# Two neighbouring 128x512 squares turned by one 128x1024 DVE instruction in an attention layer

## The chip, the cores and the metric

One Trainium2 chip, one core. The metric is the device time of one execution in microseconds (us), from the first to the last instruction of the program with what lies around it; a kernel's time is the median of its runs. The engines are named as in the profile: PE (matrix products), PEld (its weight loads), DVE, ACT and POOL (elementwise work), SP (which issues the transfers here). Each takes its own instructions in a fixed order and waits at one until its inputs are there.

## What is computed

32 graphs of 512 nodes with 256 features go through four layers, each of the form `x = x + layer(relu(layernorm(x)))`. Layers 0, 1 and 3 are graph attention layers; layer 2 is attention with eight heads of width 32. The change is in layer 2:

```python
qkv = jnp.einsum('fnc,ck->fnk', x, w_qkv)
q, k, v = jnp.split(qkv, 3, axis=-1)          # H = 8 heads, D = 32
scores = jnp.einsum('fnhd,fmhd->fhnm', q, k) / jnp.sqrt(jnp.asarray(D, x.dtype))
scores = jnp.where(adj > 0, scores, -1000000000.0)
attn = jax.nn.softmax(scores, axis=-1)
t = jnp.einsum('fhnm,fmhd->fnhd', attn, v).reshape(F, N, C)
```

Everything is in 32-bit floats.

## The kernel before

**How the work is ordered.** Class `Graph` writes down, graph by graph and layer by layer, the steps of the computation as ops: an engine, a length, what is read and written, and a function `emit` that issues the instructions. `Plan.order` then makes one list of all ops of all 32 graphs (up to six are in flight), by due times made of a period and of a table of shifts (`SHIFTS`), with buffers and banks handed out on the way. The ops' lengths are numbers written in the code (0.69 us for a square's transpose). The list is then emitted op by op, and each engine's instructions are held in that order. So the order on each engine is a product of the plan; the waits come from data: an instruction waits for the last writers and readers of what it touches.

**The attention layer.** `mha` runs twice per graph (`g`, four heads each, `PACK = 4`), and in it over pairs of node blocks (`c0 = 0, 2`), each with two blocks `c` of 128 nodes. For one block, in the order of the steps:

- PE, L1347: the four heads' scores, each 128x512, into four banks of PSUM.
- per head `h`: DVE, L1367, adds the mask and takes the smallest value, from the bank into the head's part of the buffer `p`; ACT, L1378, takes the exponential in place and sums it; DVE, L1386, turns each 32x32 square of the 128x512 part in place.
- SP, L1391: one store of the block's four heads to a page in device memory (`sheet`), then L1399, four loads from it into `pT`, which bring the squares to the other partitions. Each load waits for the store to land.

After two blocks PE, L1412, multiplies `pT` with `v` (16 products, 32 instructions); ACT copies the result (L1427), PE turns it (L1435) and DVE scales it by the sums (L1441, L1442).

`p` is one buffer of 128 partitions and, per partition, four node blocks `j`, two blocks `c`, four heads and 128 elements. A head's part is four runs of 128 elements; the parts of heads `h - 1` and `h` are neighbours, so that the two together are four runs of 256.

**Around it.** In steady state an engine's list mixes the layers of several graphs. Names that occur below: L586 and L587 (DVE, statistics of a layernorm), L791 (DVE, the masked maximum of a graph attention layer), L832 (DVE) and L840 (ACT, exponential) for its probabilities, L821 (POOL, bias), L859 (PE, a product with ones for the mean of a layer's rows), L694 (ACT, eviction with bias and relu), L704 (PE, a projection whose input L694 makes), L683 (PE, another projection), L720 (PE, rows made by transposes), L896 (DVE, the end of an elu), L1206, L1210 and L1297 (DVE, additions), L1523 (PE, products into a bank of four heads' sums), L1149 (DVE, reciprocals of sums), L809 (POOL, small arithmetic).

Only the heads that share a bank or buffer tie these layers together: PE can't write a bank of PSUM before DVE or ACT has read what was there.

The part of `mha` that is touched:

```python
def tile(h=h, c=c, p=p):
    return p[:, :, c % 2, h, :]
...
def emit(tile=tile):
    squared = tile().rearrange("p j (l i) -> p j l i", i=SQUARE)
    dve.transpose(squared, squared)

self.op("dve", 0.69, [part], [part, [(self, "done", n % 2, h)]], emit)
```

Of the kernel before, what the change touches and what calls it, by code (L numbers as in the profile page):

```python
# [50 lines left out]
SQUARE = 32  # L51
# [357 lines left out]
def adj_preln_kernel(  # L409
# [118 lines left out]
    pe, act, dve, pool = nc.tensor, nc.scalar, nc.vector, nc.gpsimd  # L528
    plan = Plan()

    def held(what, which):
        return [(what, which)]
# [10 lines left out]
    class Graph:  # L543
# [785 lines left out]
        def mha(self, g, qT, kT, v, y):  # L1329

            heads = [slice(h * MHA_DIM, (h + 1) * MHA_DIM) for h in range(PACK)]

            low = self.small(f"lows{g}", NC, PACK)
            sums = self.small(f"sums{g}", NC, PACK)
            rinv = self.small(f"rinvs{g}", NC, PACK)
            squares = P // SQUARE
            for c0 in range(0, NC, 2):

                p = Quad(NC, 2, PACK, P)
                sheet = Buffer("sheet", NC, 2, PACK * P)  # L1340
                pT = Quad(squares, 2, PACK, P)
                for c in (c0, c0 + 1):
                    sc = [Buffer("bank", N) for _ in range(PACK)]

                    def emit(c=c, sc=sc):
                        for h, d in enumerate(heads):
                            pe.matmul(  # L1347
                                sc[h].ap,
                                qT[d, g, c * P : (c + 1) * P],
                                kT[d, g, :],  # L1350
                                start=True,
                                stop=True,
                            )

                    n = g * NC + c
                    before = [(self, "done", n % 2, h) for h in range(PACK)]
                    reads = [qT.part(g), kT.part(g), before]
                    parts = [(p, c % 2, h) for h in range(PACK)]
                    self.op("pe", 1.14, reads, [*sc, parts], emit)
                    for h in range(PACK):  # L1360
                        part = [parts[h]]

                        def tile(h=h, c=c, p=p):
                            return p[:, :, c % 2, h, :]

                        def emit(h=h, c=c, sc=sc, tile=tile):
                            dve.tensor_tensor_reduce(  # L1367
                                tile(),
                                sc[h].ap.rearrange("p (j f) -> p j f", j=NC),
                                mask_bias[:, c, :].rearrange("p (j f) -> p j f", j=NC),  # L1370
                                -MHA_SCALE, HIGHEST,
                                op0=ALU.add, op1=ALU.min, accum_out=low[:, c, h : h + 1],
                            )

                        self.op("dve", 0.77, [sc[h], held("mask", c)], [part, low], emit)
                        self.op(
                            "act", 0.82, [part, low], [part, sums],
                            lambda h=h, c=c, tile=tile: act.activation(  # L1378
                                tile(), tile(), AF.Exp, scale=-1.0,
                                bias=low[:, c, h : h + 1], accum_out=sums[:, c, h : h + 1],  # L1380
                            ),
                        )

                        def emit(tile=tile):
                            squared = tile().rearrange("p j (l i) -> p j l i", i=SQUARE)
                            dve.transpose(squared, squared)  # L1386

                        self.op("dve", 0.69, [part], [part, [(self, "done", n % 2, h)]], emit)
                    self.transfer(
                        [parts], [[(sheet, c % 2)]], 1024,  # L1390
                        lambda c=c, p=p, sheet=sheet: nc.sync.dma_start(  # L1391
                            sheet[:, :, c % 2, :],
                            p[:, :, c % 2].rearrange("p j h f -> p j (h f)"),
                        ),
                    )
                    for to in range(squares):

                        def emit(c=c % 2, to=to, pT=pT, sheet=sheet):
                            nc.sync.dma_start(  # L1399
                                pT[to * SQUARE : (to + 1) * SQUARE, :, c].rearrange(  # L1400
                                    "p l h f -> p l (h f)"
                                ),
                                sheet[:, to, c].rearrange("(l p) f -> p l f", p=SQUARE),
                            )

                        self.transfer([[(sheet, c % 2)]], [[(pT, c % 2, to)]], 256, emit, True)
                acc = Buffer("bank", 2 * P)

                def emit(acc=acc, pT=pT):
                    for j in range(NC):  # L1410
                        for h, d in enumerate(heads):
                            pe.matmul(  # L1412
                                acc[d, :],
                                v[:, j, g * P + d.start : g * P + d.stop],
                                pT[:, :, :, h, j * SQUARE : (j + 1) * SQUARE].rearrange(
                                    "p l c i -> p c l i"
                                ),
                                start=(j == 0),
                                stop=(j == NC - 1),
                            )  # L1420

                reads = [(pT, c, to) for c in range(2) for to in range(squares)]
                r = Buffer("row", 2, P)
                self.op("pe", 1.97, [v, reads], [acc, r], emit)
                self.op(
                    "act", 0.4, [acc], [r],
                    lambda acc=acc, r=r: act.activation(  # L1427
                        r.ap.rearrange("p c i -> p (c i)"), acc.ap, AF.Copy
                    ),
                )  # L1430
                back = Buffer("bank", 2, PACK, MHA_DIM)

                def emit(r=r, back=back):
                    for i in range(2):
                        pe.transpose(back[:, i, :, :], r[:, i, :], ident)  # L1435

                self.op("pe", 0.27, [r], [back], emit)

                def emit(c0=c0, back=back):
                    cs = slice(c0, c0 + 2)  # L1440
                    dve.reciprocal(rinv[:, cs, :], sums[:, cs, :])  # L1441
                    dve.tensor_mul(  # L1442
                        y[:, cs, g * P : (g + 1) * P].rearrange("p c (h d) -> p c h d", h=PACK),
                        back.ap,
                        rinv[:, cs, :, None].to_broadcast([P, 2, PACK, MHA_DIM]),
                    )

                self.op("dve", 1.0, [back, sums], [rinv, y], emit)
# [199 lines left out]
```

## Time and profile before

| | |
|---|---|
| runs (3) | 4419.26, 4421.39, 4423.37 us; median 4421.39 |
| the profiled execution | 4422.42 us, of which its span 4420.6 |
| instructions in the span | 69315 |
| mean granted clock of PE | 0.979 |
| L1367, DVE, mask of one head | x1024, mean 674 ns |
| L1378, ACT, exponential of one head | x1024, mean 719 ns |
| L1391, store to the sheet | x256, 1024 KB, 5.3 us to landing |
| L1399, loads from it | x1024, 256 KB, 5.4 us to landing |
| L1412, PE | x4096, mean 395 ns |

How to read it: a page of the profile has a busy time per engine, a line of tenths for 40 equal slices of the span, and groups of instructions: line, engine, operation, what is written and read with its shape, count, busy time in us, mean ns of one, the idle time of the engine just in front of them, and what ended that idle time. A record of DVE is longer than the distance to the next one's start where two follow each other without a wait, since their ends overlap. A timeline lists instructions in order of time with the start (us from the span's start), length, engine, line and operation; "x4" is four merged; in brackets stands the idle time in front and what ended it. A view of waits sums who waited for whom. "Granted clock" is the share of full speed that PE's clock was given.

### The profile page before, as it was taken

The numbers are of one execution on the slowest core, as the hardware profiler recorded it, in microseconds if no ns is written. First come the engines' busy times: TensorE is split into PE (matmuls) and PEld (weight loads), VectorE is DVE, ScalarE is ACT, GpSimd is POOL, SyncE is SP. The second block draws the span as 40 slices with busy tenths as digits, with TensorE's granted clock in tenths as the row PEclk, the third lists the DMA queues.
The fourth block names the chain that finished last, engine by engine and source line by source line (L and its number), as shares of the span: only waits on it lengthen the run. The fifth ranks groups of instructions, "written<-read, shape, count | busy, mean of one in ns | idle before, by whom it ended". The sixth has DMA issues, their size and how long they took to land. (4 is left out here: it accounts for less than half of the span.)

```text
span 4420.6 us, 69315 instructions
## 1 busy us (share of the span) xinstructions
PE 4170.8 (94%) x21648; PEld 2583.3 (58%) x21648; DVE 3662.7 (83%) x9016; ACT 2924.3 (66%) x6309; POOL 3034.1 (69%) x3119
## 2 busy tenths in 40 slices
PE   6999999999999999999999999999999999999765
PEld 3656556665566666566666556666656666655332
DVE  3577888888888888888888888888889888888873
ACT  2556666777676667667667767666766766676653
POOL 1424766777776677776677777667777766777677
PEclk9999999999999999999999999999999999999877
DMA  3287667766767766766777667677667677766760
GB/s 121 84 226 218 187 190 220 218 202 181 215 199 211 224 200 201 204 204 194 222 215 204 201 200 211 194 224 210 205 205 206 192 217 219 201 200 186 231 175 29
DMA packets 441504, 867.22 MB, mean 196 GB/s; under 512 B 35248, under 2 KB 119728, under 8 KB 441136
## 3 DMA queue, kind: packets, MB, share of 16 engines
q1 hardware_dynamic: 439520, 862.78, 66.4%
q8 instruction: 173, 2.83, 0.3%
q14 instruction: 195, 1.60, 0.1%
q10 hardware_dynamic: 1616, 0.01, 0.0%
HBM read 443.23 MB, written 419.43 MB: 195 GB/s over the span
## 5 line engine op out<-in xcount | busy, mean ns | idle before, releaser
L1386 DVE STREAM_TRANSPOSE cells<-cells 128x512 f32<-128x512 f32 x1024 | 702.4, 698 | 148.8 <-ACT cells L1378 148.5
L1378 ACT ACTIVATE cells<-cells,smalls 128x512 f32<-128x512 f32 x1024 | 736.1, 719 | 114.0 <-DVE smalls L1367 105.8
L1367 DVE CUSTOM_DVE_ANT_0 cells<-bank,mask_bias 128x512 f32<-128x512 f32 x1024 | 686.9, 674 | 21.6 <-PE bank L1347 20.6
L821 POOL TENSOR_TENSOR cells<-mask_biasT,row 128x1024 f32<-128x1024 bf16 x320 | 682.3, 2155 | 16.2 <-ACT row L730 16.2
L791 DVE CUSTOM_DVE_ANT_0 masked<-bank,mask_bias 128x512 f32<-128x512 f32 x768 | 520.5, 678 | 71.1 <-PE bank L720 64.7
L683 PE MATMUL bank<-cells,mlp_sb 128*128 128x512 f32 x1024 | 473.1, 600 | 19.8 <-DMA cells<-page 13.2
L704 PE MATMUL bank<-fc_sb,cells 128*128 128x256 f32 (+1 forms) x2048 | 474.7, 381 | 1.5 <-DVE smalls L1367 0.8
L927 PE MATMUL bank<-cells 128*128 128x260 f32 x2048 | 465.1, 383 | 1.1 <-ACT cells L840 0.9
L603 ACT ACTIVATE cells<-cells,smalls 128x256 f32<-128x256 f32 x768 | 408.1, 592 | 74.7 <-POOL smalls L596 49.7
L1159 PE MATMUL bank<-cells 128*128 128x512 f32 x1024 | 450.9, 597 | 0.0
L927 PEld LDWEIGHTS bank<-cells 128*128 128x128 f32 x2048 | 387.9, 190 | 87.1 <-issue 24.9
L840 ACT ACTIVATE cells<-cells,smalls 128x512 f32<-128x512 f32 x512 | 348.5, 726 | 114.7 <-DVE cells L832 114.6
L704 PEld LDWEIGHTS bank<-fc_sb,cells 128*128 128x128 f32 x2048 | 376.9, 189 | 76.5 <-DVE cells L1442 19.0
L586 DVE BATCH_NORM_STATS2 smalls<-cells 128x6 f32<-128x256 f32 x768 | 311.3, 405 | 110.4 <-POOL cells L1222 101.3
L883 ACT ACTIVATE cells<-cells 128x512 f32<-128x512 f32 (+1 forms) x256 | 188.1, 735 | 292.9 <-DVE cells L946 111.3
L832 DVE SCALAR_TENSOR_TENSOR cells<-bank,smalls,cells 128x512 f32<-128x512 f32 x512 | 354.1, 740 | 30.5 <-POOL cells L821 27.0
L720 PEld LDWEIGHTS bank<-ident,smalls 128*128 128x128 f32 x2176 | 254.3, 141 | 212.6 <-issue 84.2
L720 PE MATMUL bank<-ident,smalls 128*128 128x128 f32 x2176 | 325.9, 284 | 54.2 <-POOL smalls L809 30.0
L1159 PEld LDWEIGHTS bank<-cells 128*128 128x128 f32 x1024 | 194.1, 193 | 230.2 <-issue 228.7
L1484 POOL TENSOR_TENSOR cells<-cells 128x1024 f32<-128x1024 f32 x128 | 302.3, 2372 | 19.2 <-PE bank L1502 8.4
L683 PEld LDWEIGHTS bank<-cells,mlp_sb 128*128 128x128 f32 x1024 | 186.0, 191 | 218.5 <-issue 170.3
L1347 PE MATMUL bank<-cells 32*128 32x512 f32 x2048 | 305.8, 644 | 5.7 <-DVE smalls L1367 4.8
(141 smaller groups left out, 8503.9 us busy)
## 6 DMA issues: line engine op xcount, KB each, us to landing
sheet<-cells SPq DMA_DIRECT2D x256, 1024.0 KB, 5.3
cells<-sheet SPq DMA_DIRECT2D x1024, 256.0 KB, 5.4
page<-cells SPq DMA_DIRECT2D x256, 512.0 KB, 3.4
cells<-page SPq DMA_DIRECT2D x192, 512.0 KB, 6.1
cells<-in_x_dram SPq DMA_DIRECT2D x64, 512.0 KB, 7.3
cells<-page SPq DMA_DIRECT2D x256, 128.0 KB, 2.9
out_dram<-cells SPq DMA_DIRECT2D x32, 512.0 KB, 5.4
mlp_sb<-in_L_gnn_mlp_w_dram SPq DMA_DIRECT2D x2, 512.0 KB, 6.7
```

Source lines behind the costliest of these rows:

```text
L603: lambda c=c: act.activation(xn[:, c, :], src[:, c, :], func, bias=off[:, c : c + 1], scale=rstd[:, c : c + 1],),
L683: lambda k=k, s=s, i=i, m=m, mm=mm: pe.matmul(mm.ap, w[:, k, cols + m * P : cols + (m + 1) * P], s.rows(i), start=(k == 0), stop=(k == nk ...
L704: pe.matmul(mm[:, :n], src[k // 2].nodes(k % 2, c), w[:, k, cols : cols + n], start=(k == 0), stop=(k == nk - 1),)
L720: pe.transpose(bc[:, c * P : (c + 1) * P], col(c).to_broadcast([P, P]), ident)
L791: lambda c=c: dve.tensor_tensor_reduce(masked, f2_ps.ap, bias[:, c, :], 1.0 - ALPHA, FLOOR, op0=ALU.add, op1=ALU.max, accum_out=top[:, c : ...
L821: lambda half=half: pool.tensor_add(p[half].ap, biasT[:, 2 * half : 2 * half + 2, :], w_row[:, None, :].to_broadcast([P, 2, N]),),
L832: lambda j=j, ph=ph, i=i: dve.scalar_tensor_tensor(ph[:, i, :], f1_ps.ap, term(2)[:, j : j + 1], ph[:, i, :], op0=ALU.max, op1=ALU.add,),
L927: pe.matmul(mm[:, :w1], p[j // 2][:, j % 2, c * P : (c + 1) * P], v[:, j, :], start=(j == 0), stop=(j == NC - 1),)
L1159: pe.matmul(mm.ap, h1[jh][:, i, m * P : (m + 1) * P], p[jh][:, i, :], start=(jh + i == 0), stop=(jh + i == 2),)
L1367: dve.tensor_tensor_reduce(tile(), sc[h].ap.rearrange("p (j f) -> p j f", j=NC), mask_bias[:, c, :].rearrange("p (j f) -> p j f", j=NC), - ...
L1378: lambda h=h, c=c, tile=tile: act.activation(tile(), tile(), AF.Exp, scale=-1.0, bias=low[:, c, h : h + 1], accum_out=sums[:, c, h : h + 1],),
L1386: dve.transpose(squared, squared)
```

## The change

For every odd head, one transpose turns the squares of the two heads `h - 1` and `h`; for an even head the op stays in the plan with its length, its reads and its writes, but issues nothing.

```diff
-                        def emit(tile=tile):
-                            squared = tile().rearrange("p j (l i) -> p j l i", i=SQUARE)
-                            dve.transpose(squared, squared)
+                        def emit(h=h, c=c, p=p):
+                            if h % 2:
+                                two = p[:, :, c % 2, h - 1 : h + 1, :].rearrange(
+                                    "p j h (l i) -> p j (h l) i", i=SQUARE
+                                )
+                                dve.transpose(two, two)
 
                         self.op("dve", 0.69, [part], [part, [(self, "done", n % 2, h)]], emit)
```

The ops' lengths, reads and writes are what they were, so the plan makes the same list. 1024 instructions of 128x512 become 512 of 128x1024. The odd head's instruction stands at the odd head's place in the list, wherever the even head's place is. The lines below the change move by three (L1389 is the new transpose, L1394 the store, L1402 the loads, L1415 the product).

## The prediction

> **What bounds the kernel now.** First the page, then the busy times of the engines by stage. The first fence has PE and the turned squares from the page; the second has three stages (start:end, length, then the busy time and instructions of PE, PEld, DVE, ACT and POOL, granted clock, DMA).
>
> ```profile
> PE 4170.8 (94%) x21648; PEld 2583.3 (58%) x21648; DVE 3662.7 (83%) x9016; ACT 2924.3 (66%) x6309; POOL 3034.1 (69%) x3119
> ...
> L1386 DVE STREAM_TRANSPOSE cells<-cells 128x512 f32<-128x512 f32 x1024 | 702.4, 698 | 148.8 <-ACT cells L1378 148.5
> ```
> ```profile
> 0.00:640.00 640.00, 568.55 (x2657) 359.19 (x2658) 430.86 (x1104) 347.72 (x733) 277.30 (x318) 0.97 0.59 172
> 640.00:3920.00 3280.00, 3221.53 (x17034) 2007.20 (x17034) 2868.78 (x7022) 2289.14 (x4970) 2393.64 (x2444) 1.00 0.70 206
> 3920.00:4420.00 500.00, 380.75 (x1962) 216.91 (x1958) 363.02 (x892) 287.39 (x608) 363.13 (x359) 0.87 0.57 165
> ```
>
> From 640 to 3920 us PE works 3221.5 of 3280 us (98.2%), DVE 87%. This is three quarters of the span: 26 rounds of one graph each, 129.2 to 134.1 us from one L1412 of graph g to that of g+1. PE takes its instructions in a fixed order, so in these rounds DVE's time costs nothing until a result comes later than PE needs it, and then PE loses all of the lateness. DVE's saving is not the question; DVE's order is. I therefore read the waits of PE (about 2 us a round: 20.6 us for L1297, 8.6 for L1149, 6.2 for L809 over the 18 rounds of 1170 to 3510) and then, row by row, DVE's timeline of one round, 2210 to 2342, and how long before PE's start each input was done.
>
> **Price of one wide instruction.** The trace has no 128x1024 transpose. The nearest rows are two narrow ones back to back, and L896, a 128x1024 f32 instruction from SBUF to SBUF:
>
> ```profile
> 3196.50 1.28 DVE L1386 STREAM_TRANSPOSE cells<-cells 128x512 f32<-128x512 f32 x2
> ```
> ```profile
> 3227.22 1.21 DVE L896 SCALAR_TENSOR_TENSOR cells<-cells 128x1024 f32<-128x1024 f32 x1
> ```
>
> L896 with 512 elements takes 0.68 at its shortest, so 512 more elements cost 0.53. The wide transpose is then 0.70 + 0.53 = 1.23 us, against 1.28 for the pair: merging saves some 0.06 us, 512 times 0.06 = 33 us of DVE in the whole run. Bounds of the wide one: 1.21 (L896) and 2 x 0.70 = 1.40 (no overlap at all). I take 1.23, since L896's two sizes show the slope directly and the transpose's own row shows the fixed part.
>
> The Trainium skill's "Perfetto Trace Analysis" (Identifying the Most-Contended Engine) says that matmul busy time is a bad measure of how near TensorE is to its limit, and that weight loads and useful work should be read instead; DVE is read by occupancy. Weight loads fill 61% of the middle stage, so by this rule DVE at 87% is the engine to shorten, and the sum would be a gain, 4422 - 33 = 4389. I go by the waits instead: PE's order is fixed, and it has no room whatever it does with its time.
>
> **What the change moves.** Every head keeps its place in DVE's order, but an even head's place issues nothing and the odd head's takes both. At an even place whatever follows starts 0.60 us earlier (the start to start of two narrow ones); after the odd place it is 0.53 later than that. Where DVE runs on without a wait the two cancel to -0.06. Two things break this. First, a wait between the two places eats the earliness and leaves +0.53. Second, the order of the four heads isn't always 0, 1, 2, 3: in 94 of 512 pairs the odd place comes first, so DVE is 0.53 late until the even one. In these 94 the even head's exponential was over at least 2.3 us before the odd place, so the change adds no new wait. On PE, ACT, POOL and SP the instructions and their order stay. Per round I find two places where the lateness meets PE.
>
> *Place one.* Heads go 0, 2, 3, 1. DVE waits for head 3's exponential, and both wide instructions come after that wait (columns: start us, length, engine, line):
>
> ```profile
> 2333.55 0.71 DVE L1386 STREAM_TRANSPOSE cells<-cells 128x512 f32<-128x512 f32 x1 [0.79 <-ACT cells L1378]
> 2334.34 0.43 DVE L586 BATCH_NORM_STATS2 smalls<-cells 128x6 f32<-128x256 f32 x1
> 2334.80 0.18 DVE L587 BATCH_NORM_AGGREGATE smalls<-smalls 128x2 f32<-128x6 f32 x1
> 2334.90 0.68 DVE L1386 STREAM_TRANSPOSE cells<-cells 128x512 f32<-128x512 f32 x1
> ```
>
> Everything behind 2334.90 is late by 2 x 0.53 = 1.07. Two queues carry it to PE. (a) L832 starts at 2336.03, ACT's L840 waits for it, and ACT's L694 (2338.41, after 0.25 idle) and its twin (end 2340.28) come behind: 1.07 - 0.25 less a few hundredths = 0.75 late. PE's L704 at 2340.32 starts 0.04 after that L694, in every round: PE loses 0.75. (b) SP issues the store to the sheet at 2335.67, 0.09 after the second transpose; its loads land at 2348.01 and PE's L1412 starts at 2348.47. In 9 of 26 rounds PE already waits here (0.17 to 0.91); there it loses the full 1.07. In the other 17 L1412 starts 0.51 to 0.88 after the landing, where the waiting ones start 0.24 after it (median), so the spare time is 0.27 to 0.64, the new wait 0.43 to 0.80, and (a) has mostly paid for it. Both start from the same lateness, so the larger counts: 17 x 0.75 + 9 x 1.07 = 22.4 us.
>
> *Place two* follows at once. Heads go 1, 3, 2, 0:
>
> ```profile
> 2351.64 0.71 DVE L1386 STREAM_TRANSPOSE cells<-cells 128x512 f32<-128x512 f32 x1
> 2352.27 0.65 DVE L791 CUSTOM_DVE_ANT_0 masked<-bank,mask_bias 128x512 f32<-128x512 f32 x1
> 2352.85 0.08 DVE L791 DVE_READ_ACCUMULATOR2_ANT smalls<- 128x1 f32 x1
> 2352.85 0.70 DVE L1386 STREAM_TRANSPOSE cells<-cells 128x512 f32<-128x512 f32 x1
> ...
> 2354.07 0.68 DVE L1367 CUSTOM_DVE_ANT_0 cells<-bank,mask_bias 128x512 f32<-128x512 f32 x1
> ```
> ```profile
> 2354.90 0.46 PE L859 MATMUL bank<-row,ones 128*128 128x260 f32 x1
> ```
>
> The L791 in front (2351.02) waits for PE's L720, so DVE here starts from PE's own lateness. Both wide ones run before L1367, which is 1.07 later against PE. PE's L859 needs the bank that this L1367 reads; it starts 0.15 after it in every round. Of the 0.15 about 0.13 is spare (PE's other tight starts come 0.02 to 0.05 after their input), so PE loses 1.07 - 0.13 = 0.94, times 26 = 24.4 us. The even places at 2355.29 then give 1.20 back, too late for PE.
>
> The waits for L1297, L1149 and L809 stand behind PE's own earlier work, so I let them stay. Of the 47.3 us that DVE waits at even places nothing counts while PE is full. At the end (from 3920 us, PE 76% busy) four loads of the sheet make PE wait in turn (L1412 at 4195.95, 4221.81, 4262.37, 4296.05), and their last transposes come 0.3 to 0.5 later: +2 us, bounded by -9 (the waits of DVE at L1386 after 4000 us are 8.9) and +5. At the start PE's waits are for the first loads and the mask: 0, within 3.
>
> **Sum.** 22.4 + 24.4 + 2 = 48.8 us. The profiled execution took 4422.42 (span 4420.6 and 1.8 around it), 1.0 over the median 4421.39; so 4422.4 + 48.8 = 4471 for such an execution, and 4470 as a median.
>
> **Rivals.**
> 1. *Part of the lateness is taken up by waits that PE has anyway* (10%). For: 2 us a round are there. Against: they follow PE's work. If L1149's and L809's (14.8 us in 18 rounds, 21 us in 26) shrink to nothing: 4449. If all of it is taken up, or the price is far below 0.53: within 0.2%, 4421 (6%).
> 2. *DVE was the pace after all* (8%, faster). Its saving of 33 us shows in full: 4389. For: 87% busy, 148.8 us of waits at L1386. Against: PE 98.2%.
> 3. *The clock* (8%). The window 910 to 1170 has a granted clock of 0.99 and PE busy 251.7 us, against 256.7 at 2470 to 2730 with 1.00: a dip costs 3 to 5 us. If the new waits of 0.8 to 1.1 us bring one in every second round more, 13 x 4 = 52: 4522. It decides once a wait of about 1 us is enough; the wait for L1297, up to 1.2 us, comes every round without one. The skill's "TensorE: Matmul & The Clock Gate" (Part 1) has the clock halved after an idle window of about 3.4 us; by that rule these waits alone bring none.
> 4. *The wide one costs two* (6%): 1.40, so 0.70 for each 0.53: place one 17 x 1.08 + 9 x 1.40 = 31, place two 26 x 1.27 = 33, end 2: 4488.
>
> **Chances.** The forecast has 62%. The range 4432 to 4496 leaves out rival 2, the case of no change and most of rival 3 (8 + 6 + 5 of 100), and takes in the rest of rival 1 and the bound of rival 4. A measurement of this kernel tells about 0.2% (9 us) from no change: faster 8%, within 6%, slower 86% (62 + 10 + 8 + 6).
>
> **What would show it.** L1386's successor: 512 rows of about 1.23 us. PE's waits of the middle stage: L704 for L694 some 0.75 a round, L1412 some 0.3 to 1.1, L859 for L1367 some 0.9; a round 131 us. If L859 starts without a wait, place two is wrong (the bank is free by then); if L1412 lands no later, place one. If the rounds stay at 129 to 130, PE wasn't the pace.

## The result and the profile after

The changed kernel takes 4469.61 us (median of 4 runs, 4466.59 to 4481.93) against 4422.38 us (4 runs, 4419.26 to 4427.35) for the kernel before, measured beside it: a ratio of 1.0111, 95% interval 1.0099 to 1.0124, 47 us slower by the medians. The profiled execution has a span of 4464.8 us against 4420.6. The predicted time was 4470 us.

The page of the changed kernel, first its engines and then the new transpose among the groups:

```profile
PE 4201.6 (94%) x21648; PEld 2591.9 (58%) x21648; DVE 3603.1 (81%) x8504; ACT 2922.5 (65%) x6309; POOL 3016.1 (68%) x3119
...
L1389 DVE STREAM_TRANSPOSE cells<-cells 128x1024 f32<-128x1024 f32 x512 | 633.7, 1238 | 203.3 <-ACT cells L1378 199.7
```

The transposes became cheaper: 633.7 us of DVE's time instead of 702.4, 1.238 us for one (predicted: 1.23), and all of DVE 3603.1 instead of 3662.7. In return DVE's idle time in front of them rose from 148.8 to 203.3 us. DVE has 60 us less to do and the kernel takes 47 us more: DVE's busy time isn't what PE waits for here, its order is.

Where PE waited from 640 to 3920 us (the view of waits: line of PE that waited, what released it, us in total, times, longest), first before, then after:

```profile
PE bank L1523 <- DVE cells L1297: 28.7, 25, 1.2
PE bank L720 <- DVE smalls L1149: 16.5, 25, 3.3
```
```profile
PE bank L859 <- DVE smalls L1367: 24.8, 25, 1.0
PE bank L720 <- DVE smalls L1149: 22.7, 25, 3.0
PE bank L1526 <- DVE cells L1297: 9.3, 25, 0.6
```

The wait of L859 for L1367 is new and was predicted (24.4 us). That the wait for L1297 shrinks by 19.4 us (L1526 is the old L1523) was not, nor the 6.2 us more for L1149.

To see where the time went I set each PE instruction's start after against its start before, instruction by instruction, and call the difference PE's lateness. It is 0.3 us in the first full round, 37.1 in the last (3908 us) and 43.9 at the end. In the 26 rounds between, it changes at few places, the same ones in each round:

| place in a round | change of PE's lateness, 26 rounds | predicted |
|---|---|---|
| one: L704 behind L694, with the L720 and L1415 that follow | +10.7 us | +22.4 |
| two: L859 behind L1367 | +26.7 | +24.4 |
| L1526 (L1523 before) behind L1297 | -20.2 | 0 |
| three: L1347 behind ACT's L663 | +8.3 | - |
| L720 behind L1149 | +11.8 | - |
| sum | +37.3 | +46.8 |
| after 3908 us | +6.8 | +2 |

(Places with less than 1 us are left out.) At place two and at L1526 the change is nearly the same in every round, 0.9 to 1.1 and -0.5 to -1.0 us. At L720 behind L1149 it is not: it goes from -3.5 to +5.3 us a round. 9.7 us of it fall in nine rounds, those in which PE's clock was granted at half for some us in one of the two kernels; the other 17 together add some 2. One execution of each kernel was profiled, so how far this row would differ in another execution isn't known.

Between the two profiled executions this is 44.2 us of span, predicted 48.8. The total was nearly right and its parts were not: what was counted too high and what was missed cancel, and that is luck. The experiments are about these.

### The profile page after: what moved, and what is told of

It is laid out like the page before. It is cut to its first block, busy times and chain, and to the rows that moved or that the text cites. A ratio compares the mean times of both kernels' runs of the same rounds, so it can differ in the third digit from the quotient of the medians.

```text
span 4464.8 us, 68837 instructions
## 1 busy us (share of the span) xinstructions
PE 4201.6 (94%) x21648; PEld 2591.9 (58%) x21648; DVE 3603.1 (81%) x8504; ACT 2922.5 (65%) x6309; POOL 3016.1 (68%) x3119
## 3 DMA queue, kind: packets, MB, share of 16 engines
q14 instruction: 192, 1.56, 0.1%
## 5 line engine op out<-in xcount | busy, mean ns | idle before, releaser
L1389 DVE STREAM_TRANSPOSE cells<-cells 128x1024 f32<-128x1024 f32 x512 | 633.7, 1238 | 203.3 <-ACT cells L1378 199.7
L1367 DVE CUSTOM_DVE_ANT_0 cells<-bank,mask_bias 128x512 f32<-128x512 f32 x1024 | 687.8, 678 | 55.6 <-PE bank L1347 54.3
L704 PE MATMUL bank<-fc_sb,cells 128*128 128x256 f32 (+1 forms) x2048 | 474.7, 381 | 2.2 <-DVE smalls L791 1.3
L704 PEld LDWEIGHTS bank<-fc_sb,cells 128*128 128x128 f32 x2048 | 376.9, 189 | 77.2 <-DVE cells L1445 19.1
L586 DVE BATCH_NORM_STATS2 smalls<-cells 128x6 f32<-128x256 f32 x768 | 311.4, 406 | 102.8 <-POOL cells L1222 96.2
L720 PE MATMUL bank<-ident,smalls 128*128 128x128 f32 x2176 | 330.5, 286 | 57.9 <-DVE smalls L1149 28.4
L720 PEld LDWEIGHTS bank<-ident,smalls 128*128 128x128 f32 x2176 | 254.3, 142 | 223.7 <-issue 103.3
L1347 PE MATMUL bank<-cells 32*128 32x512 f32 x2048 | 316.8, 645 | 6.4 <-DVE smalls L1367 5.1
```

The costliest lines, as they stand in the source:

```text
L704: pe.matmul(mm[:, :n], src[k // 2].nodes(k % 2, c), w[:, k, cols : cols + n], start=(k == 0), stop=(k == nk - 1),)
L720: pe.transpose(bc[:, c * P : (c + 1) * P], col(c).to_broadcast([P, P]), ident)
L1347: pe.matmul(sc[h].ap, qT[d, g, c * P : (c + 1) * P], kT[d, g, :], start=True, stop=True,)
L1367: dve.tensor_tensor_reduce(tile(), sc[h].ap.rearrange("p (j f) -> p j f", j=NC), mask_bias[:, c, :].rearrange("p (j f) -> p j f", j=NC), - ...
L1389: dve.transpose(two, two)
```

## The experiments

In the listings of these kernels a line number may stand 3 to 6 higher than in the kernel before; in the text I name it as in the kernel before (L1386 transpose, L1391 store, L1523, L1297), and in brackets as the view shows it where it differs. Ratios are to the kernel before, run on the same chip: 4417.2 us for the first four runs, 4415.09 for the next four, 4420.06 for the last two. The other columns are the changes of PE's lateness in the 26 rounds, as in the table above; the last two rows are given to the whole us.

| run | ratio, 95% interval | one | two | L1523 | three | L720 |
|---|---|---|---|---|---|---|
| the change | 1.0111, 1.0099 to 1.0124 | 10.7 | 26.7 | -20.2 | 8.3 | 11.8 |
| narrow_one | 1.0068, 1.0053 to 1.0083 | -1.3 | 27.8 | -19.6 | 9.8 | 3.9 |
| narrow_two | 1.0096, 1.0081 to 1.0111 | 8.2 | 3.2 | 1.4 | 8.0 | 7.4 |
| narrow_three | 1.0041, 1.0026 to 1.0056 | -1.4 | 0 | 4.2 | 8.0 | -3.4 |
| only_two | 1.0013, 1.0004 to 1.0023 | 0 | 27.6 | -21.9 | 0 | -0.3 |
| moved | 1.0061, 1.0044 to 1.0078 | 1.1 | 29.8 | -24.1 | 11.1 | -2.8 |
| second_place | 1.0101, 1.0086 to 1.0116 | 7.9 | 2.6 | 2.5 | 9.0 | 6.3 |
| narrow_far | 1.0059, 1.0044 to 1.0074 | -1.0 | 0 | 4.9 | 0 | 11.6 |
| quiet | 1.0005, 0.9995 to 1.0015 | -3.0 | 0 | 0 | 0 | -2.7 |
| split_wide | 1.0107, 1.0092 to 1.0122 | 10 | 26 | -13 | 7 | 11 |
| split_spread | 0.9947, 0.9932 to 0.9962 | -1 | 0 | -26 | 0 | -1 |

The first kernels differ in which of the eight blocks (g, c) of a graph have the wide transpose. Their edit on the changed kernel is this, with another condition for `wide` in each:

```diff
-                        def emit(h=h, c=c, p=p):
-                            if h % 2:
+                        def emit(h=h, c=c, p=p, tile=tile, wide=(g, c) != (1, 0)):
+                            if not wide:
+                                squared = tile().rearrange("p j (l i) -> p j l i", i=SQUARE)
+                                dve.transpose(squared, squared)
+                            elif h % 2:
```

### Place two alone narrow, place two alone wide

The run narrow_two has that edit as it stands: block (1, 0), the one of place two, is narrow.

> Two 128x512 transposes again in the block of place two (g = 1, c = 0), wide ones everywhere else. Both theories expect that PE's wait of L859 for L1367 (25.8 us in 26 rounds with the change) is gone. Theory 'taken back': PE's lateness of place two is mostly given back at L1523, whose wait for L1297 fell from 27.8 to 9.7 us with the change, because that wait follows POOL (L870 runs beside L1210) and not PE; without place two that wait comes back, and the time falls by only 26 x (1.01 - 0.77) = 6 us, to 4464 (4460 to 4468). Rival 'each term for itself': the time falls by 26 x 1.0 = 26 us, to 4444.

The run only_two turns it round, `wide=(g, c) == (1, 0)`.

> The wide transpose in the block of place two alone (g = 1, c = 0), 128x512 everywhere else. Both theories expect L859 to wait for L1367 in every round, 26 us in all. 'Taken back': L1523's wait for L1297 falls by 0.8 to 1.0 us a round at the same time, and the kernel takes 4422 to 4430. 'Each term for itself': 4422 + 26 = 4448.

Taking the wide transposes out of place two brought 0.15% at most (1.0111 to 1.0096, and the two intervals overlap), although the wait of L859 fell from 24.8 to 1.8 us; putting them there alone cost 0.13% (1.0013, interval 1.0004 to 1.0023), although that wait was there in full. By their ratios both fit 'taken back' and neither fits the rival, which expected 4444 and 4448 us. Both times the wait of L1523 (L1529) stood on the other side of the scale:

```profile
PE bank L1529 <- DVE cells L1297: 30.1, 25, 1.5
...
PE bank L859 <- DVE smalls L1367: 1.8, 10, 0.2
```
```profile
PE bank L859 <- DVE smalls L1367: 26.7, 26, 1.1
...
PE bank L1529 <- DVE cells L1297: 7.4, 23, 0.4
```

The first fence is narrow_two, the second only_two. PE loses 1.03 us at L859 in every round and, some 26 us later, at L1523, finds that the wait it used to have there is shorter by nearly as much. So the wait for L1297 doesn't stand behind PE's own work. What it does stand behind is in the timeline of one round (start, length, engine, line), before and after:

```profile
1204.33 1.89 POOL L870 TENSOR_TENSOR cells<-row,alone 128x1024 f32<-128x1024 f32 x1
1204.99 1.77 DVE L1210 SCALAR_TENSOR_TENSOR cells<-cells 128x512 f32<-128x512 f32 x1
...
1209.64 1.06 PE L1523 MATMUL bank<-cells,ones 128*32 128x512 f32 x8 [1.16 <-DVE cells L1297]
```
```profile
1204.84 1.89 POOL L870 TENSOR_TENSOR cells<-row,alone 128x1024 f32<-128x1024 f32 x1 [0.65 <-DVE smalls L944]
1206.29 0.98 DVE L1210 SCALAR_TENSOR_TENSOR cells<-cells 128x512 f32<-128x512 f32 x1
...
1210.16 1.06 PE L1526 MATMUL bank<-cells,ones 128*32 128x512 f32 x8 [0.38 <-DVE cells L1297]
```

L1210 lasts 1.77 us in the first fence and 0.66 where it runs alone. It runs beside POOL's L870, and it ends at 1206.76 and 1207.27, in both 0.54 us after the end of L870 (1206.22 and 1206.73), whether it started 0.66 or 1.45 after L870 did. After the change L1210 starts 1.30 later, POOL only 0.51, and the end goes by POOL: DVE's lateness is cut to 0.51 and PE waits 0.38 instead of 1.16. So far this is a reading of two timelines; the run split_spread below tests it.

### Place one narrow

The run narrow_one: `wide=(g, c) != (0, 3)`, place one is narrow, all else as in the change.

> Two 128x512 transposes again in the block of place one (g = 0, c = 3), wide ones everywhere else. Both theories expect that the store to the sheet there and PE's L704, L720 and L1412 lose no time against the kernel before. Rival 'each term for itself': the 0.5 us a round that place one cost comes off, 13 us, to 4457. Theory 'taken back': the same 13 us or somewhat more, 4445 to 4457, since PE then reaches L1523 only with the 1.0 us of place two, which that wait can take up whole.

It is 0.43% faster than the change (1.0068 against 1.0111), about 19 us: 12 at place one and 8 at L720, in the trace. The two theories lie too close together for this run to tell them apart: 13 us less than the change would be 1.0082, inside the interval. Place one of a round, before and after:

```profile
1297.94 0.68 ACT L694 ACTIVATE cells<-bank,mlp_bc 128x512 f32<-128x512 f32 x1
...
1298.65 1.04 PE L704 MATMUL bank<-hand_sb,cells 128*128 128x259 f32 x4
```
```profile
1294.48 1.21 DVE L1389 STREAM_TRANSPOSE cells<-cells 128x1024 f32<-128x1024 f32 x1
...
1299.36 0.67 ACT L694 ACTIVATE cells<-bank,mlp_bc 128x512 f32<-128x512 f32 x1
...
1299.56 1.23 PE L704 MATMUL bank<-hand_sb,cells 128*128 128x259 f32 x4
1300.08 0.30 PEld L704 LDWEIGHTS bank<-hand_sb,cells 128*128 128x128 f32 x2 [0.33 <-ACT cells L694]
```

L704 starts 0.91 later, which is PE's lateness already there. L694 ends at 1300.03 instead of 1298.62, 1.41 later, so 0.50 beyond that. But L704 began before L694 had ended in both kernels: its first products read the part that L694 made one instruction earlier, and only the later weight load waits (the bracket in the last line). So PE loses 0.19 (1.23 against 1.04), not L694's 0.50. With what follows at L720 and L1412 it is 0.4 a round.

### All three places, and the third one

The run narrow_three: `wide=(g, c) not in ((0, 3), (1, 0), (1, 2))`.

> Two 128x512 transposes again in three blocks: place one (g = 0, c = 3), place two (g = 1, c = 0), and a third found in the trace of the changed kernel (g = 1, c = 2), where the wide transpose stands in front of the L1367 that frees a bank for L1347, 0.4 us a round. Wide ones in the other five blocks of a graph. Both theories expect the steady rounds of the kernel before: 4420 to 4432, with what the start and the end change. A rival that puts the loss down to the wide instruction itself, wherever it stands, expects five eighths of it: 4452.

4436.89 us, 1.0041: 0.4% stays, more than expected, though the rival's 4452 is out. The trace shows place one and two gone, and 8.0 us at a place that I had put down to the wrong block: L1347 behind L663. SP's queue, ACT and PE there, first before and then in narrow_three (where L1391 is L1397, the store of the output L1594 instead of L1588):

```profile
1230.29 0.53 SPq L1391 DMA_DIRECT2D sheet<-cells  x1
1230.92 0.57 SPq L1588 DMA_DIRECT2D out_dram<-cells  x1
...
1236.45 0.60 ACT L663 ACTIVATE cells<-bank 128x512 f32<-128x512 f32 x1 [1.55 <-DMA out_dram<-cells]
...
1236.96 1.25 PE L1347 MATMUL bank<-cells 32*128 32x512 f32 x8
```
```profile
1231.77 0.53 SPq L1397 DMA_DIRECT2D sheet<-cells  x1
1232.39 0.57 SPq L1594 DMA_DIRECT2D out_dram<-cells  x1
...
1237.96 0.60 ACT L663 ACTIVATE cells<-bank 128x512 f32<-128x512 f32 x1 [1.99 <-DMA out_dram<-cells]
...
1238.04 1.70 PE L1347 MATMUL bank<-cells 32*128 32x512 f32 x8
```

PE is 1.08 late here (1238.04 against 1236.96). The store of block (0, 1) goes out 1.48 later, since its last transpose is wide, so 0.40 beyond PE's lateness. SP issues the finished output of another graph next, right behind it; its buffer comes free 0.4 later, L663 waits 1.99 instead of 1.55 for it, and L1347, whose bank L663 empties, is drawn out to 1.70. Nothing of this is in the attention layer's own chain: it is what stood behind the store on SP. So the layers are tied together by more than shared banks and buffers, which is all that the part on the kernel before names: by SP's queue here, and by POOL's L870 beside DVE's L1210 above.

The run narrow_far tests that block: `wide=(g, c) not in ((0, 1), (0, 3), (1, 0))`.

> Narrow transposes in the blocks (g=0, c=1), (g=0, c=3) and (g=1, c=0), wide in all the others; against the run with three narrow blocks before it, (0,1) takes the place of (1,2). Theory (what was left there comes from the block (0,1): its late transpose holds the store of line 1391 on SP, the store of the finished output is queued right behind it, the buffer it reads comes free late, and ACT's line 663 and PE's line 1347 of the next round wait): the 0.3 us a round behind line 1347 go, 8 us, and the time is 4422 to 4431 against 4437 there. Rival (the block (1,2) or the mass of wide transposes as such): 4437 or more.

The place went (0 instead of 8.0 us), so the block is the right one. The time didn't follow: 4442.08 us, 1.0059, above what the theory allowed and no better than narrow_three (the intervals overlap), since PE lost 11.6 us at L720 where narrow_three had gained 3.4. That place is not settled. What is seen: L1149 stands on DVE behind L586, which waits for POOL's L1222, which adds a page that SP loads (L973) right behind the store of block (1, 3). In some rounds that load lands too late. POOL's wait for it, before and in the change:

```profile
POOL cells L1222 <- DMA cells<-page: 11.6, 8, 3.1
```
```profile
POOL cells L1222 <- DMA cells<-page: 17.1, 11, 2.8
```

It was 14.8 us (11 times) in narrow_far, 8.4 (6) in narrow_three and 7.7 (5) in moved. With block (1, 3) wide the store goes out 0.25 late; but that was so in narrow_three too, which lost nothing here. In these kernels PE's stretches of half clock all stand at L720's wait: 7 windows of 3.4 us in the middle stage of the change and in narrow_far, 4 before and in narrow_three. (In narrow_one, second_place and moved one stretch each stands at L1347.) The wait comes first: in the kernel before and in the change it had begun 1.0 to 4.1 us before the clock fell, all ten times. But four waits of 1.2 to 2.4 us passed in the change without such a stretch. PE waits over 1 us there in ten rounds of the change and in five of the kernel before; why in those is open.

### What costs: the place or the width

The run moved keeps the narrow instructions but issues both at the odd head's place, as two.

```diff
-                        def emit(tile=tile):
-                            squared = tile().rearrange("p j (l i) -> p j l i", i=SQUARE)
-                            dve.transpose(squared, squared)
+                        def emit(h=h, c=c, p=p):
+                            for k in (h - 1, h) if h % 2 else ():
+                                squared = p[:, :, c % 2, k, :].rearrange(
+                                    "p j (l i) -> p j l i", i=SQUARE
+                                )
+                                dve.transpose(squared, squared)
```

> The transposes stay narrow (two of 128x512 a pair, as before), but both are issued at the place of the odd head, where the change issues its one of 128x1024. Theory (the place costs, not the width of the instruction): DVE does there two instructions of 0.70 us, 1.40 us against the change's 1.24, so every later end on DVE comes 0.1 to 0.2 later than in the change: PE's wait of the line 859 matmuls for line 1367 about 1.1 to 1.2 us a round (1.0 in the change), 28 to 31 us in all, and a time of 4470 to 4480. Rival (the wide instruction itself is what costs, its form or its length in one piece): no wait there and a time near the kernel before, 4417 to 4425.

The wait of L859 came as expected of the place, 27.7 us (24.8 in the change), and PE's lateness rises by 1.15 a round there:

```profile
PE bank L859 <- DVE smalls L1367: 27.7, 25, 1.1
...
PE bank L1526 <- DVE cells L1297: 5.2, 22, 0.3
```

So the rival, which expected no wait, is out. The whole time missed all the same: 4441.25 us, 1.0061, half of the change's loss. By the table the largest difference to the change is L720's, 14.6 us, the place that isn't settled; L1526 took back 3.9 more, and places two and three cost some 3 more each. The rest is place one, where moved loses 1.1 us against 10.7. DVE there, in moved and in the change:

```profile
1285.94 0.71 DVE L1389 STREAM_TRANSPOSE cells<-cells 128x512 f32<-128x512 f32 x1
1287.90 0.71 DVE L1389 STREAM_TRANSPOSE cells<-cells 128x512 f32<-128x512 f32 x1 [1.26 <-ACT cells L1378]
```
```profile
1292.79 1.25 DVE L1389 STREAM_TRANSPOSE cells<-cells 128x1024 f32<-128x1024 f32 x1 [1.89 <-ACT cells L1378]
```

Head 2's narrow one runs before DVE's wait for head 3's exponential, and the wide one does both heads behind it. So here the joining itself costs something, not only the place: two narrow ones leave DVE 0.59 late there instead of 0.86, L694 0.23 late instead of 0.50, and L704 loses nothing instead of 0.18. Together the two kernels give PE's spare time at this place: some 0.3 us behind L694. The prediction had counted 0.04, the distance to an instruction that doesn't need L694 for its first half.

In the run second_place the transpose is wide everywhere, but at whichever of the pair's two places comes later (`seen` is a set made for each block).

```diff
+                    seen = set()
...
-                        def emit(tile=tile):
-                            squared = tile().rearrange("p j (l i) -> p j l i", i=SQUARE)
-                            dve.transpose(squared, squared)
+                        def emit(h=h, c=c, p=p, seen=seen):
+                            if h // 2 in seen:
+                                k = h - h % 2
+                                two = p[:, :, c % 2, k : k + 2, :].rearrange(
+                                    "p j h (l i) -> p j (h l) i", i=SQUARE
+                                )
+                                dve.transpose(two, two)
+                            seen.add(h // 2)
```

> The wide transpose is issued at whichever of the pair's two places comes later in the order, so in the sequence (1,0,2,3) of the block g=1, c=0 and in (0,2,3,1) of the block g=0, c=3 nothing else that was behind it is now ahead of it for the sake of a pair already complete. Theory: the wait of line 859 for line 1367 is gone (26 us in the change), the places in the blocks g=0, c=3 and g=0, c=1 stay, and the wait of line 1523 for line 1297 comes back to 28 to 31 us, as in the run with the block g=1, c=0 narrow: 4455 to 4463. Rival (what the block g=0, c=3 costs comes from where its late half is issued, not from the joining): at most 4440.

4461.32 us (1.0101), as the theory had it; the rival's 4440 is out. The waits:

```profile
PE bank L1529 <- DVE cells L1297: 31.2, 25, 1.5
```

L859 isn't among them any more, and the 31.2 us at L1523 (L1529) are back: the prediction's largest term can be removed by a better place for the instruction, and that is worth 0.1% (1.0111 to 1.0101), no more than the noise.

Last of these, the run quiet has the wide transpose only in the two blocks behind which no place was found, `wide=(g, c) in ((0, 2), (1, 1))`.

> The wide transpose only in the blocks g=0, c=2 and g=1, c=1, narrow in the six others: out go the three places (0,3), (1,0) and (0,1), the block (1,3), behind whose store to the sheet SP queues the load that POOL's line 1222 waits for, the block (1,2) on SP ahead of it, and the block (0,0), behind which DVE's line 944 is late for POOL's line 870. Theory (every loss is a place where a late half holds something that PE needs soon; the width costs nothing by itself): a time within 0.2% of the kernel before, 4408 to 4424, the wait of line 1523 at 28 to 30 us. Rival (each wide block costs its share whatever lies behind it): a quarter of the change's 47 us, 12 us, so 4427, and below that the clock's accidents.

4422.5 us against 4420.06, a ratio of 1.0005 (0.9995 to 1.0015): no difference, and the rival's 12 us (0.27%) lie outside the interval. PE's lateness in the 26 rounds goes from 1.5 to -2.4. In these two blocks the wide transpose costs PE nothing, and brings nothing: 128 instructions take 158.9 us in place of 256 at 0.698, and DVE's busy time in all falls from 3662.7 to 3653.3 us, of which nothing shows.

### POOL's multiplication in halves

If L1210 is held by POOL's L870, then the 28.7 us that PE waits at L1523 in the kernel before can be had without any transposes. The run split_spread is the kernel before with L870 as two instructions:

```diff
-                lambda: pool.tensor_mul(
-                    y.ap,
-                    mean[:, None, :C].to_broadcast([P, NC, C]),
-                    alone[:, :, None].to_broadcast([P, NC, C]),
-                ),
+                lambda: [
+                    pool.tensor_mul(
+                        y[:, s, :],
+                        mean[:, None, :C].to_broadcast([P, 2, C]),
+                        alone[:, s, None].to_broadcast([P, 2, C]),
+                    )
+                    for s in (slice(0, 2), slice(2, 4))
+                ],
```

> The kernel before with one edit that has nothing to do with the transposes: POOL's multiplication of line 870 as two instructions of half its size, the result the same. Theory (DVE's line 1210 lasts until 0.55 us behind POOL's line 870 because the two run side by side, and PE's line 1523 waits 28 us in all for the line 1297 behind it, which is why lateness of PE up to 0.8 us a round cost the change nothing there): the mean of line 1210 falls from 1132 ns to 800 or below, most of the wait of line 1523 goes, and the time is 4393 to 4405. Rival (line 1210 is held by something else, or both halves of POOL hold it as the whole did): line 1210 keeps its 1.1 us, the wait its 28 us, and the time is 4415 to 4425.

4391.91 us (4390.67 to 4396.27), a ratio of 0.9947, interval 0.9932 to 0.9962: 23 us faster than the kernel before, and the fastest here. A group of the page and, from the view of PE's waits, the line that was the largest (L1523 is L1526 here, L1210 L1213):

```profile
L1213 DVE SCALAR_TENSOR_TENSOR cells<-cells 128x512 f32<-128x512 f32 x64 | 51.3, 802 | 2.2 <-DMA cells<-in_x_dram 1.1
```
```profile
PE bank L1526 <- DVE cells L1300: 2.0, 4, 1.6
```

The mean fell from 1132 to 802 ns, and the wait from 28.7 to 2.0 us, although POOL needs more for the two halves, 2 x 1.13 us, than for the whole, 1.90. L1210 starts in the first half and ends 0.55 behind the end of that.

The run split_wide has the change and the halves together, that is, this diff on the changed kernel.

> The change and the halved multiplication of line 870 together. Theory (in the change 20 us of PE's lateness were taken back at the line behind DVE's line 1297, since that stood behind POOL and not behind PE; with line 870 in halves this wait is gone before the change comes, 2.0 us left in all, and nothing can be taken back): the change costs 44 + 20 = 64 us on top of the halved version's 4392, so 4448 to 4464, a ratio of 1.007 to 1.011 to the kernel before; the halving brings at most 20 us to the change. Rival (the two edits add, the halving worth 23 us in either): 4440 to 4447.

4470.79 us against 4420.06, 1.0107. By the ratio that is within what the theory said, by the time above it: the halves bring the change nothing at all, where the theory allowed up to 20 us and the rival 23. Against the halved kernel the change costs 1.0107 / 0.9947, 1.6%, some 70 us. But the wait that should have been gone wasn't (L1529 is L1523):

```profile
PE bank L1529 <- DVE cells L1300: 16.2, 25, 1.0
```
```profile
1209.08 2.04 POOL L871 TENSOR_TENSOR cells<-row,alone 128x512 f32<-128x512 f32 x2 [0.63 <-DVE smalls L947]
1210.44 1.22 DVE L1213 SCALAR_TENSOR_TENSOR cells<-cells 128x512 f32<-128x512 f32 x1
```

The timeline shows why: with the change DVE comes later against POOL, L1213 starts 1.36 after the first half, when that is over (1.04), and is held by the second half, to 0.54 behind its end (1211.12). PE's lateness is still taken back here, by 13 us against the kernel before (20 in the change). So the number came near for another reason than the theory gave: the halves free L1210 only if it meets the first one.

## Why the prediction was right, and where it wasn't

**Price of one wide instruction**: right, 1.238 us (1.23).

**PE as the pace, DVE's saving worth nothing**: right. DVE worked 60 us less and the kernel took longer; in quiet 9 us less changed nothing. Rival 2 is out. The rule of the Trainium skill that the prediction quoted ("Perfetto Trace Analysis", Identifying the Most-Contended Engine), used with PE's weight loads (61%) against DVE's occupancy (87%), would have made DVE the engine to shorten; here PE's waits told the truth, and that use of the rule didn't. Its other measure for PE, useful work, was not worked out.

**Place two**: right in mechanism and size. PE loses 1.03 us a round at L859 (0.94 predicted):

```profile
1314.76 0.68 PE L859 MATMUL bank<-row,ones 128*128 128x260 f32 x2 [0.99 <-DVE smalls L1367]
```

**Place one**: right in mechanism, mis-sized. 22.4 us were predicted and 10.7 measured. DVE was 0.86 late, not 1.07, since a gap of 0.16 behind one of the transposes took a part; L694 was 0.50 late, not 0.75; and "PE loses 0.75" was the wrong step, since L704 starts on the part that was ready before, and loses 0.18. The loads' way (b), with 9 x 1.07, was late by no more than what (a) had paid, but for 2.7 us.

**"The waits for L1297, L1149 and L809 stand behind PE's own earlier work, so I let them stay"**: the step that failed. For L1297 the last in time before it was DVE's L1210, and L1210 ended when POOL let it, 0.55 us after L870. The profile before had it: L1210's two instructions of a round lasted 1.77 and 0.66 us, the same shape. Of the 1.0 us that place two made PE late, 0.78 a round was taken back there, 20.2 us. That is rival 1, with another wait than the two it named. (In narrow_two, without place two, the same wait was 30.1 us: place one's 8.2 us were not taken back there.)

**What was not seen at all**: place three (8.3 us), where SP has another layer's store behind the late one, and L720's (11.8, of which the cause is open). I had followed DVE's lateness along the data of the attention layer, and SP's queue only to its own loads.

**The end**: 6.8 us instead of 2, outside the bounds given (-9 to 5). No run was made for it; it stays open. In quiet, whose time is that of the kernel before, PE's lateness rises by 3 us over the same stretch.

**Rival 3, the clock**: not as it was put. None of the stretches of half clock stands at the new waits of about 1 us (L859), and there are three windows more, not 13. At half the clock, three windows of 3.4 us cost PE at most 3 x 1.7 = 5 us of work. But the rounds that have such a stretch in one kernel or the other carry most of L720's 11.8 us, waits included. They came with single waits of 1.1 to 3.3 us, shorter than the idle window of about 3.4 us in the rule quoted beside this rival.

**Rival 4**: out, by the row of 1238 ns.

So 48.8 us were predicted and 44.2 found between the profiled executions, because 20.2 that were taken back, and 11.7 too many at place one, made room for 8.3 + 11.8 unseen in the middle, 4.8 more at the end and 2.3 more at place two. The direction didn't hang on one place: even with place two gone (second_place, narrow_two) the kernel is 1% slower.

## What to carry to other kernels

Where one engine with a fixed order is nearly always at work, joining two instructions of another engine is worth nothing by the time it saves; look at what the joined one pushes back, on its own engine and in the queue that waits for it (SP's next transfer may belong to another layer). The joined one also waits for the later of its two inputs, and loses the time in which the first half could have run. Before you let an existing wait stand or count on it, follow it one step further back than its releaser: if that ends by another engine, here POOL, a delay in front of it is taken back there, and the wait itself can be had for less. Where an instruction's length differs from round to round, or from place to place, at the same shape, ask what holds it: here that row was worth 23 us.

## What the hardware showed that was not expected

DVE's L1210 (two operands in SBUF) ended 0.54 to 0.55 us behind the end of the POOL instruction that was running when it started, in each of the 25 rounds of the middle stage of before, the change, narrow_three, quiet and split_wide, and in split_spread (26 rounds) behind the first half; its start varied from 0.34 to 2.14 us after POOL's. (In moved, where it starts 1.56 us or more after POOL, it ends 0.55 to 0.62 behind.) It lasted 0.77 to 1.78 us so, and 0.66 alone. The Trainium skill's "SBUF — State Buffer" (SBUF: two separate sides) has it that such a DVE instruction and a GpSimd one that reads SBUF take a port pair in turns, whichever starts first holding it for its whole instruction while the other is blocked. The runs agree with that. POOL was held as well: in split_spread, where DVE gets in between, the second half took 1.49 us, and 1.04 in split_wide, where it was first.
